# Preparing a stage's first weights, bias and input inside the stage before it, in tiles that stage has used up

## The chip, the cores and the metric

The kernel runs on one core of a Trainium2 chip. The metric is device time in microseconds (us) of one execution. The engines are TensorE (PE; its weight loads are PEld), VectorE (DVE), ScalarE (ACT), GpSimd (POOL) and SyncE (SP); SP issues nearly all transfers, in order. Each engine takes its instructions in one fixed order and waits on semaphores.

## The reference

Two transformer-like layers over one sequence of 4096 rows and 256 channels, in float32. What matters here is layer 0, and that layer 1 follows it.

```
x = L0_attn_x                                  # (1, 4096, 256)
sa, ca, ga, sb, cb, gb = modulation(L0_c)      # six rows of 256
h = layernorm(x) * (1 + ca) + sa
x = x + ga * attention(h)                      # 16 heads of 16, causal; ... @ Wo + bo
h = layernorm(x) * (1 + cb) + sb
shared = swiglu(h @ w_shared_in) @ w_shared_out
probs  = softmax(h @ w_gate + gate_bias)       # 8 experts, the top 2 kept as weights wd
hid    = swiglu(h @ w1_shared)
x = x + gb * (shared + sum_e wd[e] * (hid @ w2[e]))
... layer 1: a gated delta rule and a quantised matmul ...
```

The constants `ga` and `gb` are folded into weights by the kernel: `Wo` and `bo` are multiplied by `ga`, `w_shared_out` and `w2` by `gb`.

## The kernel before

**Stages.** Setup computes the modulation rows on PE and DVE (pool `modw`). The attention follows (`attention`, L249): `attn_inputs` goes through 8 blocks of 512 rows, normalises them, forms queries, keys and values, and writes queries and keys to DRAM in high and low parts; then `interleave` (L309) runs 32 steps, each one group g of 4 heads with one block T of 512 queries. After that the mixture (`mixture`, L672) and layer 1.

**Keys in the attention.** `kts[i][p]` (L255) are four tiles of 128x4096: group g's keys are in `kts[g % 2]`, p is the pair of heads. So `kts[0]` holds groups 0 and 2, `kts[1]` groups 1 and 3. The steps are laid out in the list at L276 to L280; the last six are (3,2), (3,3), (3,7), (3,6), (3,5), (3,4), all with group 3, and group 2's last step is (2,4) just ahead of them. All four tiles and the values `vall` are filled with a constant by POOL (L256 to L259), then the causal mask is brought by a transfer that POOL issues (L264) and copied twice by DVE (L268).

**A step.** PE forms logits for row maxima (tile `m`, two buffers), DVE reduces them (`mx`, L526, one 128x1024 tile at a time), the maxima go back as query rows through SP (`q<-mrow`), and PE forms the logits again (`e`), ACT takes the exponential (L640), PE multiplies with the values (`o`). Maxima run ahead of the steps that need them; the query loads (`q<-qd`) run four steps ahead. At a step's end `ot` is copied by ACT, transposed, and divided by DVE (`rec`, `o`, L659 and L660).

**The mixture.** `mixture_weights` (L704) loads all weights and the input into new tiles and prepares them. Weights that must be exact are split in two halves by `halves` (L692): DVE cuts the low bits away (`cut`, L696), ACT copies the high part, POOL subtracts to get the low part (L700). That is done for `w_shared_in` and `w1_shared` (tile `win`) and for 8 pieces of `w2` (tile `w2f`, two buffers), each piece multiplied by `gb` first (L745). POOL also adds the bias to every block of x (`biased`, L772). `before_experts(b)` (L751) makes for one block of 512 rows: the heads' transposes, the projection with `Wo` and its sum into x (L789), statistics with a root on POOL (L798), normalisation on ACT (L804), transposes, gate and the choice of two experts (`chosen`), and 8 products for the two hidden layers. `experts(b)` does the shared product and 4 pairs of experts for each of 4 tiles of 128 rows, on PE, and DVE adds them into x (L911, L927). Block b + 1's pieces are mixed into block b's experts by a list of slots.

**What sets the order.** Python order is program order. A scheduler places instructions on each engine by a simulated clock and by program order as priority; what goes through `mm`, `tp`, `mma` (PE) and `dv` (mostly DVE) keeps its program order among itself, the rest may be moved ahead as far as its inputs and buffers allow. A pool opened after another is closed may take the same bytes, and then the first use waits for the last use of what lay there. The wait is by pool: in the program before, the pool `attn` lies at bytes 56352 to 162592 of each partition and `modw` at 23584 to 56480; `kt00` itself lies at 93088.

**Layer 1** begins with some 20 loads on SP (from `Wq`), 24 DVE operations that make `conv` matrices, a quantised weight turned by PE (L1086), and the first block's normalisation, whose transposes (L1143) follow on PE.

Of the kernel before, what the change touches and what calls it, by code (L numbers as in the profile page):

```python
# [7 lines left out]
F32 = mybir.dt.float32  # L8
# [9 lines left out]
P = 128  # L18
# [81 lines left out]
class _Net:  # L100
# [150 lines left out]
    def attention(self):  # L251
# [3 lines left out]
        self.kts = [[self.t(ap_, [P, S], f"kt{i}{p}", F32R) for p in range(2)] for i in range(2)]  # L255
# [26 lines left out]
        with ExitStack() as c:  # L282
# [7 lines left out]
            self.small = e(tc.tile_pool(name="asmall", bufs=2))  # L290
            self.ps_e = e(tc.tile_pool(name="ps_e", bufs=3, space=PSUM))
# [24 lines left out]
    def interleave(self):  # L316
# [16 lines left out]
        values, tail = None, None  # L333
        for i, (g, T) in enumerate(steps):
# [5 lines left out]
            ahead(need[i])  # L340
            for n, (logits, made) in enumerate(self.weighted(g, T)):
# [8 lines left out]
                values = made  # L350
        values(0)
# [321 lines left out]
    def mixture(self):  # L673
        nc, tc = self.nc, self.tc
        with ExitStack() as c:
# [5 lines left out]
            self.mixture_weights()  # L681
            for f in self.before_experts(0):
                f()
            for b in range(NB):
# [7 lines left out]
    def halves(self, full, high, low, ordered=True):  # L692

        nc = self.nc
        cut = self.t(self.ms, [P, 512], "cut")
        ins = nc.vector.tensor_scalar(cut.bitcast(I32), full.bitcast(I32), HIGH, None, ALU.bitwise_and)  # L696
        if ordered:
            self.dv(ins)
        nc.scalar.copy(high, cut)
        nc.gpsimd.tensor_tensor(low, full, cut, ALU.subtract)  # L700

    def mixture_weights(self):
        nc, a, wp = self.nc, self.a, self.mw
        m = self.mods[0]  # L704
        w = self.w = {}
        xs = a["L0_attn_x"].rearrange("o (n p) c -> p (o n) c", p=P)

        def load(b):
            nc.sync.dma_start(out=self.x[:, 4 * b : 4 * b + 4, :], in_=xs[:, 4 * b : 4 * b + 4, :])

        w["o"] = self.weight(wp, a["L0_attn_Wo"], C, "wo")
        load(0)
        bo = self.rows(wp, a["L0_attn_bo"], C, "bo")

        nc.vector.tensor_tensor(
            w["o"], w["o"], m["ga"].unsqueeze(1).to_broadcast([P, 2, C]), ALU.mult
        )
        nc.vector.tensor_tensor(bo, bo, m["ga"], ALU.mult)
        w["bo"] = bo
        w["g"] = self.weight(wp, a["L0_ffn_w_gate"], 8, "wg")  # L720
        w["gbias"] = self.rows(wp, a["L0_ffn_gate_bias"], 8, "gbias")
        w["in"] = []
        for name, tag in (("L0_ffn_w_shared_in", "wsi"), ("L0_ffn_w1_shared", "w1s")):
            full = self.t(self.ms, [P, 2, 512], "win")
            nc.sync.dma_start(out=full, in_=a[name].rearrange("(k p) n -> p k n", p=P))
            t = self.t(wp, [P, 2, 2, 512], tag, F32R)
            for k in range(2):
                self.halves(full[:, k], t[:, 0, k], t[:, 1, k], ordered=False)
            w["in"].append(t)

        w["so"] = self.weight(wp, a["L0_ffn_w_shared_out"], C, "wso")
        nc.gpsimd.tensor_tensor(
            w["so"], w["so"], m["gb"].unsqueeze(1).to_broadcast([P, 2, C]), ALU.mult
        )
        gb2 = m["gb"].unsqueeze(1).to_broadcast([P, 2, C])
        w["2"] = self.t(wp, [P, 2, 2, 8, C], "w2", F32R)
        for k in range(2):
            for e in range(0, 8, 2):
                es = slice(e, e + 2)
                full = self.t(self.ms, [P, 2, C], "w2f")  # L740
# [7 lines left out]
        for b in range(1, NB):  # L748
            load(b)

    def before_experts(self, b):  # L751
# [22 lines left out]
        def attended(k):  # L774
# [4 lines left out]
            if k == 0 and b == 0:  # L779
                biased(0)  # L780
# [920 lines left out]
```

## Time and profile before

| | us |
|---|---|
| median of 3 runs (lowest, highest) | 3238.63 (3233.23, 3240.27) |
| the profiled execution | 3230.99 |
| its span | 3229.2 |
| busy: PE, DVE, ACT, POOL | 2924.4, 2239.3, 1786.7, 454.0 |
| granted TensorE clock, mean | 0.907 of full speed |
| last reduction step's `rec` of group 2 (step (2,4)) | at 1511.13 |
| attention's last `ot` copy | at 1834.64 |
| first expert pair of the mixture | 1907.63 to 1909.16 |
| last expert product of the mixture | to 2234.8 |

Busy times say which engine works most, not what holds the end. The chain of waits does that: followed back from the last instruction, it names at each time what the next piece of work waited for. The timeline shows each engine's instructions in order of time, with the idle time before them and what ended it. The table by windows shows the same stretch for all engines, with the clock granted to PE.

### The profile page before, as it was taken

The numbers are of one execution on the slowest core, as the hardware profiler recorded it, in microseconds if no ns is written. First come the engines' busy times: TensorE is split into PE (matmuls) and PEld (weight loads), VectorE is DVE, ScalarE is ACT, GpSimd is POOL, SyncE is SP. The second block draws the span as 40 slices with busy tenths as digits, with TensorE's granted clock in tenths as the row PEclk, the third lists the DMA queues.
The fourth block names the chain that finished last, engine by engine and source line by source line (L and its number), as shares of the span: only waits on it lengthen the run. The fifth ranks groups of instructions, "written<-read, shape, count | busy, mean of one in ns | idle before, by whom it ended". The sixth has DMA issues, their size and how long they took to land.

```text
span 3229.2 us, 61627 instructions
## 1 busy us (share of the span) xinstructions
PE 2924.4 (91%) x24988; PEld 1740.1 (54%) x24988; DVE 2239.3 (69%) x3923; ACT 1786.7 (55%) x3866; POOL 454.0 (14%) x698
## 2 busy tenths in 40 slices
PE   4877999999999999999999769997788998889877
PEld 3444444444444444444444358886667677667755
DVE  4565688888888888888887266666247557755665
ACT  0211577777877777777888622221555455545521
POOL 3222100000000000000000141111223223323312
PEclk8777799999999999999999979998889798989855
DMA  3433100003000020000000110001011011101000
GB/s 123 140 129 110 30 10 11 12 7 51 7 12 12 13 49 6 12 10 8 11 2 2 52 49 1 1 1 27 10 19 19 11 24 22 20 13 23 18 19 11
DMA packets 143084, 89.05 MB, mean 28 GB/s; under 512 B 102928, under 2 KB 120848, under 8 KB 142224
## 3 DMA queue, kind: packets, MB, share of 16 engines
q1 hardware_dynamic: 142656, 85.04, 10.3%
q8 instruction: 197, 3.23, 0.4%
q14 instruction: 87, 0.71, 0.1%
q0 software_dynamic: 144, 0.07, 0.0%
HBM read 51.05 MB, written 33.55 MB: 26 GB/s over the span
## 4 chain that ended last, share of the span: by engine, by line
PE 67%; DVE 19%; ACT 6%; issue 3%; POOL 3%; DMA 2%; SPq 1%; DVEq 0%; POOLq 0%; ACTq 0%
PE o L168 16%; PE e L168 13%; DVE mx L526 9%; PE m L168 9%; PE f L1152 9%; PE b L1152 6%; PE a L1152 4%; PE f L168 2%; PE w L168 2%; DVE step L1384 1%; ACT kk L1281 1%; PE ps L427 1%; DVE T L1391 1%; ACT e L640 1%; DVE by L1246 1%
## 5 line engine op out<-in xcount | busy, mean ns | idle before, releaser
L640 ACT ACTIVATE e<-e 128x512 f32<-128x512 f32 (+1 forms) x2176 | 1151.5, 583 | 319.6 <-PE e L168 285.7
L526 DVE TENSOR_REDUCE mx<-m 128x2 f32<-128x1024 f32 (+3 forms) x1088 | 1202.0, 1129 | 171.2 <-PE m L168 158.9
L168 PE MATMUL o<-e,vall 128*32 128x256 f32 (+2 forms) x9216 | 692.4, 375 | 5.4 <-ACT ot L617 5.4
L168 PE MATMUL e<-q,kt 50*128 50x512 f32 (+3 forms) x2688 | 571.3, 438 | 0.3 <-ACT e L640 0.3
L168 PE MATMUL m<-kt,q 48*128 48x512 f32 (+3 forms) x2688 | 481.1, 379 | 7.4 <-DVE mx L526 4.9
L168 PEld LDWEIGHTS e<-q,kt 50*128 50x128 f32 x2688 | 249.9, 185 | 431.8 <-issue 257.8
L168 PEld LDWEIGHTS o<-e,vall 128*32 128x32 f32 x9216 | 192.5, 108 | 323.8 <-issue 300.6
L168 PEld LDWEIGHTS m<-kt,q 48*128 48x128 f32 x2688 | 249.9, 192 | 85.4 <-issue 45.4
L772 POOL TENSOR_TENSOR x<-x,bo 128x1024 f32<-128x1024 f32 x8 | 19.9, 2505 | 1508.3 <-DMA x<-in_L_attn_x_dram 1508.3
L1152 PE MATMUL f<-conv,pT 128*128 128x128 f32 x1536 | 224.4, 297 | 0.0
L1152 PEld LDWEIGHTS f<-conv,pT 128*128 128x128 f32 x1536 | 200.8, 206 | 8.7 <-issue 1.4
L1152 PE MATMUL b<-w,hid 128*128 128x512 f32 x768 | 195.9, 399 | 0.0
L927 DVE SCALAR_TENSOR_TENSOR x<-b,wd,x 128x256 f32<-128x256 f32 x256 | 123.6, 483 | 66.5 <-PE b L1152 59.4
L1152 PEld LDWEIGHTS b<-w,hid 128*128 128x128 f32 x768 | 143.3, 188 | 29.9 <-POOL hid L700 0.3
L1475 ACT ACTIVATE gs<-S,gm 128x64 f32<-128x64 f32 x256 | 75.4, 340 | 117.6 <-DVE S L1503 117.3
L534 DVE TENSOR_REDUCE mx<-m 128x8 f32<-128x1024 f32 x64 | 78.4, 1225 | 71.0 <-PE m L168 70.6
L1503 DVE TENSOR_TENSOR S<-gs,w 128x128 f32<-128x128 f32 x128 | 36.5, 285 | 126.7 <-PE w L168 104.3
L168 PE MATMUL w<-S,uw 64*32 64x64 f32 x1024 | 62.8, 252 | 54.8 <-DVE S L1503 53.9
L1480 DVE TENSOR_TENSOR ut<-uw,w 32x256 f32<-32x256 f32 x128 | 53.3, 416 | 80.9 <-PE w L168 79.1
L1384 DVE TENSOR_TENSOR step<-T,Ls 128x126 f32<-128x126 f32 (+22 forms) x248 | 79.4, 320 | 27.1 <-DMA Ls<-dL 21.9
L1152 PE MATMUL f<-frac,hT 128*128 128x128 f32 x640 | 90.9, 295 | 0.0
L168 PEld LDWEIGHTS w<-S,uw 64*32 64x32 f32 x1024 | 38.6, 122 | 94.8 <-DVE S L1503 70.1
(286 smaller groups left out, 3636.3 us busy)
## 6 DMA issues: line engine op xcount, KB each, us to landing
q<-qd SPq DMA_DIRECT2D x128, 96.0 KB
kt<-kd SPq DMA_DIRECT2D x12, 768.0 KB
x<-in_L_attn_x_dram SPq DMA_DIRECT2D x16, 512.0 KB
kd<-high SPq DMA_DIRECT2D x32, 256.0 KB
qd<-high SPq DMA_DIRECT2D x32, 256.0 KB
kd<-full SPq DMA_DIRECT2D x16, 256.0 KB
qd<-full SPq DMA_DIRECT2D x16, 256.0 KB
Ls<-dL SPq DMA_DIRECT2D x64, 64.0 KB
```

Source lines behind the costliest of these rows:

```text
L168: self.nc.tensor.matmul(out, lhsT, rhs, start=start, stop=True, skip_group_check=skip)
L427: nc.tensor.matmul(ps, w[:, k, ch * P : (ch + 1) * P], hT[:, k, :], start=(k == 0), stop=(k == 1))
L526: nc.vector.tensor_reduce(mx[:, 2 * pair : 2 * pair + 2, s, col], ps[:, :, at : at + w], AX.X, ALU.max)
L534: nc.vector.tensor_reduce(mx[:, 2 * pair : 2 * pair + 2, :, 0], ps.rearrange("p h (s k) -> p h s k", k=P), AX.X, ALU.max,)
L640: nc.scalar.activation(e[:, 0:at], ps[:, 0:at], AF.Exp)
L927: nc.vector.scalar_tensor_tensor(x, ps[:, e, :], wd[:, s, n : n + 1], x, ALU.mult, ALU.add)
L1152: self.nc.tensor.matmul(out, lhsT, rhs, start=(k == 0), stop=(k == n - 1))
L1246: nc.vector.tensor_tensor(by[z].rearrange("p (i h) f two -> p i (h f) two", i=2), qk.rearrange("p i h (f two) -> p i (h f) two", two=2), c ...
L1384: nc.vector.tensor_tensor(step[:, 0:m, 0:n], T[:, 0:m, j].unsqueeze(2).to_broadcast([P, m, n]), Ls[:, j + 1 : 32, j].unsqueeze(1).to_broad ...
L1475: nc.scalar.activation(gs[:, pair, :], state[:, pair, :], AF.Identity, scale=gm[:, pair, c : c + 1])
L1480: nc.vector.tensor_tensor(ut[rows].rearrange("p (a b) d -> p a b d", b=2), u[rows].rearrange("p (a b) d -> p a b d", b=2), pw[rows, :, 0:1 ...
L1503: nc.vector.tensor_tensor(self.state, gs, pw[:, 0, 128:256].rearrange("p (a d) -> p a d", d=64), ALU.add)
```

## The change

Keys tiles `kts[0]` move from the attention's pool to the pool `heads`, which stays open through the mixture. When group 2 is finished, these tiles take the mixture's first data:

- `mixture_vectors` loads the gate's weights and bias into the constants' pool, and puts `Wo`, `w_shared_out`, `bo` (each multiplied on POOL) and the first block of x with `bo` added into `kts[0][1]`. Each goes through a tile `full` of a new pool `early` (two buffers): load, POOL operation, transfer into place.
- `mixture_early` returns four pieces that split `w_shared_in` and `w1_shared` into `kts[0][0]`: load, DVE cut, ACT copy, POOL subtraction.
- In the mixture, blocks 1 to 7 of x are loaded first, and the eight splits of `w2` (`split_expert`) are written out between the pieces of the first `before_experts`, after `chosen`. `w2` has two tiles, one per k.
- The bias of block b + 1 is added after `chosen(b)`, in program order; the first block's sum reads x and bias from `kts[0][1]`.

```diff
-        self.kts = [[self.t(ap_, [P, S], f"kt{i}{p}", F32R) for p in range(2)] for i in range(2)]
+        self.kts = [[self.t((self.hp, ap_)[i], [P, S], f"kt{i}{p}", F32R) for p in range(2)] for i in range(2)]
...
+            self.early = e(tc.tile_pool(name="early", bufs=2))
...
+        later, count = [], 0
...
             ahead(need[i])
+            if i == len(steps) - 4:
+                self.mixture_vectors()
+            if i == len(steps) - 2:
+                later = self.mixture_early()
...
+                count += 1
+                if later and count % 3 == 0:
+                    later.pop(0)()
+        for f in later:
+            f()
...
-            self.mixture_weights()
-            for f in self.before_experts(0):
+            xs = self.a["L0_attn_x"].rearrange("o (n p) c -> p (o n) c", p=P)
+            for b in range(1, NB):
+                nc.sync.dma_start(out=self.x[:, 4 * b : 4 * b + 4, :], in_=xs[:, 4 * b : 4 * b + 4, :])
+            self.w["2"] = [self.t(self.mw, [P, 2, 8, C], f"w2{k}", F32R) for k in range(2)]
+            for n, f in enumerate(self.before_experts(0)):
                 f()
+                if 9 <= n < 13:
+                    for k in range(2):
+                        self.split_expert(self.ms, k, 2 * (n - 9))
...
+    def mixture_vectors(self):
+        nc, a, cp = self.nc, self.a, self.const
+        m = self.mods[0]
+        room = self.kts[0][1].bitcast(F32)
+        wo, wso = (room[:, 512 * n : 512 * n + 512].rearrange("p (k n) -> p k n", k=2) for n in range(2))
+        self.x0 = x0 = room[:, 1024:2048].rearrange("p (s n) -> p s n", s=4)
+        bo = room[:, 2048:2304]
+        self.w = {"o": wo, "so": wso, "bo": bo}
+        self.w["g"] = self.weight(cp, a["L0_ffn_w_gate"], 8, "wg")
+        self.w["gbias"] = self.rows(cp, a["L0_ffn_gate_bias"], 8, "gbias")
+
+        def kept(to, src, shape, op, by):
+            t = self.t(self.early, [P, 512], "full")
+            flat = t[:, 0 : shape[0] * shape[1]]
+            wide = flat.rearrange("p (k n) -> p k n", k=shape[0])
+            nc.sync.dma_start(out=wide, in_=src)
+            nc.gpsimd.tensor_tensor(wide, wide, by.unsqueeze(1).to_broadcast([P, *shape]), op)
+            nc.sync.dma_start(out=to, in_=wide)
+
+        kept(wo, a["L0_attn_Wo"].rearrange("(k p) n -> p k n", p=P), (2, C), ALU.mult, m["ga"])
...
+        for n in (0, 2):
+            kept(x0[:, n : n + 2, :], xs[:, n : n + 2, :], (2, C), ALU.add, bo)
+
+    def mixture_early(self):
...
+                pieces.append(lambda i=i, k=k, src=src: self.split(src, w["in"][i][:, 0, k], w["in"][i][:, 1, k]))
+        return pieces
+
+    def split(self, src, high, low):
+        nc = self.nc
+        full = self.t(self.early, [P, 512], "full")
+        nc.sync.dma_start(out=full, in_=src)
+        cut = self.t(self.early, [P, 512], "cut")
+        nc.vector.tensor_scalar(cut.bitcast(I32), full.bitcast(I32), HIGH, None, ALU.bitwise_and)
         nc.scalar.copy(high, cut)
         nc.gpsimd.tensor_tensor(low, full, cut, ALU.subtract)
...
+    def split_expert(self, pool, k, e):
+        nc, w = self.nc, self.w
+        src = self.a["L0_ffn_w2"][e : e + 2, k * P : (k + 1) * P, :].rearrange("e p c -> p e c")
+        full = self.t(pool, [P, 512], "full")
+        nc.sync.dma_start(out=full.rearrange("p (e c) -> p e c", e=2), in_=src)
...
+        nc.vector.tensor_tensor(wide, wide, gb2, ALU.mult)
+        cut = self.t(pool, [P, 512], "cut")
+        nc.vector.tensor_scalar(cut.bitcast(I32), full.bitcast(I32), HIGH, None, ALU.bitwise_and)
+        high, low = (w["2"][k][:, h, e : e + 2].rearrange("p e c -> p (e c)") for h in range(2))
+        nc.scalar.copy(high, cut)
+        self.dv(nc.gpsimd.tensor_tensor(low, full, cut, ALU.subtract))
...
-            self.dv(nc.vector.tensor_tensor(xh, ps, xh, ALU.add))
+            two = slice(2 * half, 2 * half + 2)
+            old = x4 if b else self.x0
+            self.dv(nc.vector.tensor_tensor(x4[:, two, :], ps, old[:, two, :], ALU.add))
...
-            nc.gpsimd.tensor_tensor(rs, ve, self.mhalf[:, 0:4], ALU.pow)
-            biased(b + 1)
+            self.dv(nc.gpsimd.tensor_tensor(rs, ve, self.mhalf[:, 0:4], ALU.pow))
...
             self.dv(nc.vector.tensor_tensor(wd, pr, picked, ALU.mult))
+            biased(b + 1)
...
     with tc.tile_pool(name="heads", bufs=1) as hp:
+        net.hp = hp
```

## The prediction

> **What bounds the kernel now.** I read the page's overview first: PE is busy for 2924 us of a 3229.2 us span, so I looked for the places where it is not. The chain of waits and the timeline, read around the lines of the diff, show two holes, one at the start and one between attention and mixture.
>
> The chain of waits, start of the span (start, us, what). From 34.4 to 59.3 us the chain is POOL filling tiles, a small transfer and two DVE copies; PE waits.
>
> ```profile
> 34.41 13.94 POOL kt L258 x4
> 48.34 7.64 POOL vall L259
> 55.99 2.40 DMA causal<-in_const_causal_dram
> 58.41 0.49 DVE mask L268 x2
> 58.91 0.33 DVE x L148
> 59.29 2.20 PE ps L158 x8
> ```
>
> The same view from the attention's end (1834.6) to the experts. PE's first projection ends at 1842.13, and nothing of PE's is on the chain until 1886.6: the holder is the weights' splitting, three near-equal rounds of load, multiply, cut and subtract, 8.67 us apart (1854.60, 1863.27, 1871.94).
>
> ```profile
> 1838.31 7.17 DMA wso<-_L_ffn_w_shared_out_dram
> ...
> 1854.60 2.72 DMA w2f<-in_L_ffn_w_dram
> ...
> 1857.41 1.64 DVE w2f L745
> ...
> 1859.14 2.39 DVE cut L696
> ...
> 1861.60 1.65 POOL w L700
> 1863.27 2.51 DMA w2f<-in_L_ffn_w_dram
> ...
> 1882.25 0.60 DVE x L789
> ...
> 1890.26 15.63 PE a L1152 x62
> ...
> 1907.63 1.53 PE b L1152 x6
> ```
>
> The table by windows gives the granted clock (after POOL's busy time, ahead of the DMA share): half speed after the hole, full speed again only from about 1896.
>
> ```profile
> 1842.00:1844.00 2.00, 0.13 (x1) 0.00 (x0) 0.00 (x0) 0.00 (x0) 1.22 (x1) 1.00 1.05 398
> 1846.00:1848.00 2.00, 0.00 (x0) 0.00 (x0) 1.10 (x1) 0.57 (x2) 2.00 (x2) 0.50 1.09 346
> 1894.00:1896.00 2.00, 2.00 (x7) 1.52 (x6) 1.46 (x9) 1.51 (x2) 0.00 (x0) 0.50 0.00 0
> 1896.00:1900.00 4.00, 4.00 (x18) 3.29 (x17) 2.26 (x10) 1.20 (x2) 0.00 (x0) 0.95 0.00 0
> ```
>
> The DVE timeline late in the attention, where the new splits land: ten reductions back to back, 1.24 us each, no gap.
>
> ```profile
> 1512.03 12.39 DVE L526 TENSOR_REDUCE mx<-m 128x2 f32<-128x1024 f32 x10 [0.19 <-PE m L168]
> ```
>
> The timeline of PE at layer 1's start: its first matmul there, after 16.45 us of waiting.
>
> ```profile
> 2251.22 0.59 PE L1086 MATMUL f<-identb,wqb 128*128 128x128 bf16 x4 [16.45 <-issue]
> ```
>
> **Part 1, the start.** Moving kt00 and kt01 out of the attention's pool changes more than it says. In the memory map of the program before, that pool begins at byte 56352 and shares 128 bytes with the modulation's pool, which ends at 56480, so its first fill waits for the modulation (34.4). After, the pool begins at 89216 and shares none. POOL's order in the built kernel is now kt10, kt11, vall, the causal load and both mx without that wait, and only then kt00 and kt01 with it. From about 0.4 us: two fills at 3.49 (13.94 / 4) and vall at 7.64 end near 15; the masks' transfer (2.40) ends near 18. What stays behind 34.41 is two fills, 6.98, to 41.4.
> On DVE, beside a fill, a TENSOR_SCALAR of 128x2 at 34.38 lasted 3.56 us, to that fill's end, and one of 128x4 at 39.33 lasted 2.09, to 41.42, while bn_stats ran through. In the new order the two mask copies stand ahead of that first TENSOR_SCALAR. If neither is held, POOL's root starts at 41.5 and the normalised x at 42.6 instead of 58.82: 16.2 us. If the second copy (due at 34.45, just after the fill begins) is held to 37.9, the TENSOR_SCALAR is held to 41.4, the block's statistics (four times 0.39 and 0.15, then 0.16: 2.3) end at 43.7, the root (1.02) at 44.8: 14.0 us. No row has a copy beside a fill; the nearest row, that TENSOR_SCALAR, was held, so I take 14.0.
> The Trainium skill (SBUF — State Buffer, SBUF: two separate sides) says that DVE and GpSimd share one port pair, held for a whole instruction, and that a copy in a two-port mode is among those that wait. By that rule too the gain is 14.0 and the sum below 38.0; without it 16.2 and 40.2.
> The early fills also stand beside DVE's copy of scb (9.67): held to 15.1 it is still ahead of its reader on PE (16.68): 0. Everything up to the keys' loads follows the first block, with no clock of its own: the gain stays.
>
> **Part 2, preparation inside the attention.** POOL gets five multiplications or additions and four subtractions (1.26 to 1.44 each), in a stretch where it has nothing: 0. The SP queue gets nine loads and five stores. Two loads stand behind the first keys' loads, ahead of query loads that wait for later logits; two stores and two loads stand between 1490 and 1503, where SP has nothing else (issues at 1487.55 and 1503.47): 0. The rest stand behind the four query loads that end at 1505.7 and ahead of those at 1533.93. The store of bo, the second x load, two x stores and the piece loads form a series: taking 2.5 us each (the w2f rows) and 1.3 to 1.5 for each POOL step between, the first two pieces land near 1515.9 and 1517.9, and the last near 1523.4, before 1533.93: no query load is late, 0.
> DVE reaches its first cut after two reductions, at 1514.5: a wait of 1.4. Then four cuts of 0.43 (1904.07 has one alone): 3.1 in all, in the stretch without gaps. An m tile is written again 2.48 after its last writing began and is free after 0.45 + 1.23: 0.8 of slack. So 2.3, and 0.2 for semaphores: **2.5 lost**. ACT's four copies (0.57 to 0.62, 2.4) fall in the same 10 us, where ACT has 1.8 us idle (8.19 busy of 10) plus PE's delay: covered. Bounds: 0 if the transfers are quicker and PE's lead larger, 6 if the wait is 4 or cuts are held by POOL (2.39 was seen).
>
> **Part 3, the hole.** Removed from ahead of the first block: four cuts of win, eight multiplications and cuts of w2, and POOL's eight subtractions with its biases. The first x sum's second half had its input at 1842.13 and began at 1882.25. After, DVE has two gb multiplications in front (loads issued at 1834.7 and 1835.2, landed by 1837.8, 0.68 each), done by 1839.3; so it starts at 1842.2, and all to the hidden matmuls moves 40.1 us forward: 1893.27 becomes 1853.2. That is the upper bound.
> But the experts' eight splits now stand behind, in DVE's queue between the hidden blocks' products, and their loads pass through two buffers. Step by step: the first cut (after lg, 1853.4) shares its time with POOL's bias of block 1 (2.34) and ends at 1855.0; POOL's two subtractions (1.3 each) end at 1856.6 and 1858.3; the selection's 16 small DVE operations (0.225 from start to start) end at 1860.2. Then three rounds, each load 2.7, multiply 0.68, cut 0.43, subtract 1.3, semaphores 0.2, thus 5.3: with the first delayed by the selection, subtractions 3, 5, 7 end at 1863.0, 1868.4, 1873.7, and DVE's eighth cut at 1874.9. Behind it wait hid0's second product (0.69), both sl products (0.69) with their cuts (0.43): 2.9 to 1877.9, since the last PSUM tiles were filled by 1867.5. POOL's two subtractions end at 1879.6, and the first expert pair ends near 1880.6 instead of 1909.16: 28.5.
> PE stands still from 1867.5 to 1875.7. Row: 2 to 4 us after 1842.13 the clock was 0.50, and it took unbroken work from 1890.26 to about 1896.2 to be full again. The same at half speed costs 2.9. The Trainium skill (TensorE: Matmul & The Clock Gate, Part 1: The HAM clock gate) gives one activity window of about 3.4 us; by it the loss is an estimated 1.7 (half of it) and the sum below would be 39.2. I take the row: 28.5 - 2.9 = **25.6 gained**. Bounds: with the old rounds of 8.67 each, 3 x 3.4 = 10.1 less, 15.5; without the clock's loss, 28.5.
> The biases of blocks 1 to 7 (2.34 each) were done in the hole; now one per block runs on POOL. Cover: POOL's 2.6 to 3.6 busy of 20 us in steady state; the cuts they may hold feed hid tiles used a block later: 0. If that cover failed, at most 7 x 2.34 = 16.
>
> **Part 4, layer 1.** Its weight tiles now lie where kt0 and o lay, and the first load waits for the last shared product (2228.26 to 2229.28) and not for the last expert pair (2234.8): 5.6 earlier. DVE's conv stretch (from 2241.98, waiting for taps) then starts when x and three tiles' statistics are done, 2237.5: 4.5 earlier, ending at 2247.7. But the fourth tile's statistics, the root and the first nxn now stand behind it: 0.36 + 0.30 + 0.17 + 1.01 + 0.16 + 0.52 and gaps, 2.9, to 2250.6; the transposes began at 2251.6. **0.9 gained**, bounds -2 and 4.5.
>
> **Sum.** 14.0 + 25.6 + 0.9 - 2.5 = 38.0. The profiled execution took 3230.99 (span 3229.2), so 3193.0. It is 7.6 below the median of the runs, 3238.63; for the median I say 3238.6 - 38.0 = **3200.6**.
>
> **Rivals.**
> A, the splits keep their old rounds (8.67): DVE's multiplications took 1.64 and cuts 2.39 beside POOL. Against: that was beside POOL's x biases (5.08 for two), mostly gone. 10.1 less: 3210.7.
> B, the start gives nothing, another wait taking the fill's place (the weights' loads, or kt00's fill before the first key load). Against: all those loads are issued by 18.2. 38.0 - 14.0 = 24.0: 3214.6.
> C, the attention's DVE waits a whole transfer (2.5) at each of four cuts: 10 more lost, 3210.6. The built order puts one or two reductions (1.24) between cuts, which speaks for half of that at most.
> D, slower: the clock. After the shorter pause PE's full clock could be throttled through the mixture, which is PE alone for 327 us (1907.6 to 2234.8). It decides from 38 us of loss, a clock of 327 / (327 + 38) = 0.90; at 0.85 it costs 57.7: 3258. Against: the page's granted clock is 9 tenths or more in every slice from 404 to 1857, without a pause.
>
> **How the numbers follow.** Forecast 0.62, A 0.18, B 0.08, C 0.08, D 0.03, a remainder within 0.2% 0.01. The likeliest case alone spans 3194 (16.2, 28.5, 4.5 at the start, hole and layer 1, less 5) to 3208. The range reaches A, C and part of B: 3190 to 3215. Within 0.2% (6.5 us, near what runs from 3233.23 to 3240.27 can tell) is 0.01, slower 0.03, faster 0.96.
>
> **What would show it.** Right: POOL's vall fill near 7 us and the first PE transposes at 43 to 45; ten reductions near 1500 stretched by 3 with four cuts among them; x's first sum right after its projection; three rounds of about 5.3 in the splits, PE idle for about 8 us before the experts at half clock; layer 1's first load ahead of the last pairs. Wrong: rounds over 7, a gap on PE in the attention over 6, blocks of the mixture longer than 40.9 us ((2234.8 - 1907.6) / 8), or a clock below 1.00 there.

## The result and the profile after

The changed kernel took 3188.43 us (median of 4 runs, 3182.70 to 3194.45), the kernel before 3236.78 beside it (4 runs): a ratio of 0.9851, 95% interval 0.9829 to 0.9873, so 48.4 us less. The prediction was 3200.6 with a range from 3190.0 to 3215.0; the time lies 1.6 us below the range, in the case that was forecast. The profiled execution took 3182.70 (span 3180.9) against 3230.99 (span 3229.2): 48.3 less.

The table sets both profiles side by side; the times are starts of the first or last instruction of a tile. "Again" columns are further profiles of the same two kernels, taken in the experiments.

| us from the span's start, or length of a stage | before | again | after | again | third |
|---|---|---|---|---|---|
| modulation's last row (`gb`, L242) starts | 33.80 | 30.89 | 29.95 | 29.97 | 30.17 |
| first transposes of the attention | 59.3 | 56.6 | 39.3 | 39.4 | 39.6 |
| from there to the attention's first division | 293.6 | 294.6 | 293.6 | 293.6 | 293.4 |
| first to last division of the attention | 1483.0 | 1483.0 | 1486.2 | 1485.9 | 1507.7 |
| last division to first hidden product | 57.3 | 57.3 | 16.9 | 16.9 | 16.9 |
| first hidden to first expert product | 14.1 | 14.2 | 26.1 | 26.1 | 26.1 |
| first to last expert product | 327.0 | 327.0 | 327.5 | 327.5 | 328.4 |
| last expert product to layer 1's first Wq product | 23.0 | 23.1 | 22.7 | 22.3 | 22.3 |
| from there to the end | 971.8 | 970.9 | 968.4 | 967.1 | 971.5 |

The chain of waits of the changed kernel, start of the span. The fills of 34.41 to 55.99 are gone from it; what is left of them are two DVE operations that last 3.23 and 2.00 us beside the two late fills.

```profile
19.64 3.53 PE pc L206 x32
...
29.95 0.41 DVE gb L242
30.36 0.40 DVE mask L269 x2
...
31.00 3.23 DVE bq L421
...
35.71 2.00 DVE ave L145
37.80 1.05 POOL ars L133
38.87 0.42 DVE x L148
39.34 2.20 PE ps L158 x8
```

POOL's timeline shows where those fills went: three start at once, two after the modulation.

```profile
0.73 6.96 POOL L259 MEMSET kt<- 128x4096 f32 x2 [0.29 <-POOLq L1719]
7.62 7.84 POOL L260 MEMSET vall<- 128x9184 f32 x1
...
30.55 7.13 POOL L259 MEMSET kt<- 128x4096 f32 x2 [13.92 <-issue]
```

The chain between attention and experts. The first sum into x has its second half at 1825.31, where PE's projection of 1821.49 (3.79 long) ends. What holds the experts is two rounds of load, multiply, cut and subtract that begin at 1848.88 and 1855.05, on to DVE's last cut and the hidden product behind it.

```profile
1825.31 0.70 DVE x L823
...
1848.88 2.59 DMA full<-in_L_ffn_w_dram
...
1855.05 2.62 DMA full<-in_L_ffn_w_dram
...
1858.60 0.43 DVE cut L780
1859.03 0.61 DVE hid L911
1859.68 1.22 PE b L1186 x2
```

PE's timeline there, and the table by windows (the granted clock stands after POOL's busy time): PE pauses for 6.50 us, and the clock is 0.50 until about 1862.9.

```profile
1859.68 1.22 PE L1186 MATMUL b<-kt,hid 128*128 128x256 f32 x2 [6.50 <-DVE hid L911]
```

```profile
1854.00:1856.00 2.00, 0.00 (x0) 0.00 (x0) 0.65 (x1) 0.32 (x1) 1.03 (x1) 1.00 0.37 118
1856.00:1858.00 2.00, 0.00 (x0) 0.00 (x0) 0.70 (x3) 0.62 (x1) 1.29 (x1) 0.50 0.49 131
...
1860.00:1862.00 2.00, 2.00 (x9) 1.71 (x9) 1.76 (x4) 0.96 (x2) 1.53 (x2) 0.50 0.00 0
...
1864.00:1866.00 2.00, 2.00 (x10) 1.75 (x11) 0.97 (x2) 0.07 (x1) 0.00 (x0) 1.00 0.03 8
```

In the attention, DVE's first early cut waits 1.77 us for its piece (DVE's timeline), and PE then waits 1.19 (PE's timeline).

```profile
1496.62 0.43 DVE L766 TENSOR_SCALAR cut<-full 128x512 int32<-128x512 int32 x1 [1.77 <-DMA full<-n_L_ffn_w_shared_in_dram]
```

```profile
1498.24 0.50 PE L168 MATMUL e<-q,kt 50*128 50x512 f32 x1 [1.19 <-ACT e L652]
```

Layer 1's first load is issued at 2184.74, ahead of the last expert products (2189.8), and the first Wq product follows the last expert product by 22.7 instead of 23.0.

So the first profiled pair adds up as: start 20.0, attention -3.2, hole 27.8 (40.4 less before the hidden products, 12.0 and 0.5 given back behind them), layer 1's start 0.3, layer 1's body 3.4. The sum of the prediction had 14.0, -2.5, 25.6, 0.9 and nothing for layer 1's body.

### The profile page after: what moved, and what is told of

Read it like the earlier page. It is cut to its first block, busy times and chain, and to the rows that moved or that the text cites. A ratio compares the mean times of both kernels' runs of the same rounds, so it can differ in the third digit from the quotient of the medians.

```text
span 3180.9 us, 61656 instructions
## 1 busy us (share of the span) xinstructions
PE 2918.7 (92%) x24988; PEld 1732.8 (54%) x24988; DVE 2239.9 (70%) x3921; ACT 1786.7 (56%) x3866; POOL 452.4 (14%) x701
## 3 DMA queue, kind: packets, MB, share of 16 engines
q8 instruction: 197, 3.23, 0.4%
## 4 chain that ended last, share of the span: by engine, by line
PE 66%; DVE 19%; ACT 6%; issue 3%; POOL 2%; DMA 2%; SPq 1%; DVEq 0%; POOLq 0%; ACTq 0%
PE o L168 16%; PE e L168 13%; PE m L168 9%; DVE mx L538 9%; PE f L1186 9%; PE b L1186 6%; PE a L1186 4%; PE f L168 2%; PE w L168 2%; DVE step L1418 2%; ACT kk L1315 1%; DVE T L1425 1%; PE ps L439 1%; ACT e L652 1%; DVE by L1280 1%
## 5 line engine op out<-in xcount | busy, mean ns | idle before, releaser
L961 DVE SCALAR_TENSOR_TENSOR x<-b,wd,x 128x256 f32<-128x256 f32 x256 | 123.5, 482 | 61.8 <-PE b L1186 55.3
L1186 PE MATMUL a<-hs,kt 128*128 128x512 f32 x384 | 102.7, 406 | 2.2 <-DVE hid L911 2.2
```

The lines of the kernel that those rows point to most:

```text
L961: nc.vector.scalar_tensor_tensor(x, ps[:, e, :], wd[:, s, n : n + 1], x, ALU.mult, ALU.add)
L1186: self.nc.tensor.matmul(out, lhsT, rhs, start=(k == 0), stop=(k == n - 1))
```

## The experiments

Theory: the gain comes from the three places named, and what exceeds the sum is partly chance of those executions. Rivals: each of the surplus terms belongs to the change; or a place gives nothing and another gives more.

**The same two kernels again.** No edit.

> The kernel before, unchanged, profiled again. Two terms of the sum stay open: PE's second pass of column products in the modulation (32 products) took 6.62 us before and 3.53 after, and layer 1 from its first Wq product to the end took 971.8 us before (3229.2 - 2257.40) and 968.4 after (3180.9 - 2212.49). Theory 1, both vary from one execution to the next whatever the kernel: here the pass takes anything from 3.5 to 7.0, and layer 1 anything from 967 to 973. Theory 2, both belong to the program: the pass takes 6.6 again, and layer 1 971.8 within 0.5.

> The changed kernel, unchanged, profiled again. Theory 1 (the pass's speed and layer 1's 3.4 us vary from one execution to the next): the pass takes anything from 3.5 to 7.0, the first transposes start between 39 and 43, layer 1 takes 967 to 973. Theory 2 (they belong to the program): 3.53, 39.3 and 968.4 within 0.5. By both, PE's pause ahead of the experts is 6.5 again within 0.5.

The kernel before took 3228.41, and its second column pass 3.69 instead of 6.62; its layer 1 took 970.9. The chain of waits of this second profile:

```profile
20.51 3.69 PE pc L206 x32
...
30.89 0.43 DVE gb L242
...
31.50 13.94 POOL kt L258 x4
```

The changed kernel took 3188.11 (4 runs, ratio 0.9866, 0.9837 to 0.9896), with a pass of 3.51 and a layer 1 of 967.1. Theory 1 holds for the pass: one and the same kernel before has 6.62 and 3.69, and two profiles of another unchanged kernel below have 6.62 and 3.54. Over all 15 profiles of the study it is 6.6 to 7.0 in eight and 3.5 to 3.8 in seven. The modulation's end, 3.85 us earlier in the first pair, is therefore no gain of the change (3.09 of it is this pass; 0.66 is the first pass's start, 9.69 against 9.03, which lies anywhere from 8.98 to 9.96 in the 15 profiles). For layer 1 the third profile decides: 971.5 in a changed kernel, as before, and the kernel before with a pad, below, has 968.4. Its 3.4 us are chance too.

**The start alone.** 128 bytes in the kernel before, so that the pools no longer touch.

```diff
         net.o = net.t(hp, [P, NT, C], "o")
+        net.t(hp, [P, 32], "pad")
```

> The kernel before with one tile of 128 bytes behind the heads, so that the attention's tiles share no byte with the modulation's; nothing else. My theory (the shared 128 bytes alone held the fills): all four key fills and vall run from 0.7 to about 22.5, the first transposes start at 35 to 39 instead of 59.29 (fills free from the start: 33.8 for the end of the modulation at full speed or 4 later, 2.3 of statistics, 1.05 for the root, 0.5), and 20 to 24 us are gained, unless DVE's copy of scb is held by the fills to 15 or 22 and PE's row products with it (then 6 less). Rival, another wait takes the fills' place: transposes after 50, gain under 10.

3209.77 us (ratio 0.9926, 0.9902 to 0.9950): about 24 us of 3233. The chain of waits:

```profile
20.11 6.62 PE pc L206 x32
...
33.61 0.42 DVE gb L242
...
38.25 0.38 DVE x L148
38.67 1.56 PE ps L158 x5
```

With the slow pass, the transposes still start at 38.67 instead of 59.29, 20.6 earlier. So the 128 bytes held all fills (the addresses of the memory map stand in no profile; that a pad of 128 bytes is enough is what this run shows), and an edit of one line, which leaves every tile in its pool, gains more at the start than the change does: here no fill stands beside the statistics.

**The start undone.** The changed kernel with its fills, mask load and `mx` behind the modulation's last row.

```diff
+        late = self.mods[1]["gb"][:, 0:1]
+        nc.gpsimd.tensor_copy(self.vall[:, 0, 0:1], late)
+        for kt in self.kts[1]:
+            nc.gpsimd.tensor_copy(kt[:, 0:1], late)
...
+        nc.gpsimd.tensor_copy(causal[:, 0:1], late)
...
+            nc.gpsimd.tensor_copy(m[:, 0, 0, 0:1], late)
```

> The changed kernel with all fills, the mask's load and mx made to wait again for the modulation's last row (tiny POOL copies of it into each tile first), the rest as changed. My theory, the start's gain adds to the rest: the first transposes start at 53 to 59.3 (POOL fills 21.6 us from 30.4 or 34.2 on), so 14 to 20 us of the 48 are lost and the kernel takes 3202 to 3209. Rival, the later parts hide the start (something late in the kernel ends by its own clock): less than 5 lost, 3188 to 3193.

3204.28 us (7 runs; ratio 0.9916, 0.9891 to 0.9941): 16.2 above the changed kernel of the same call, inside the 14 to 20. The first transposes start at 58.11. The start's gain adds to the rest.

Its profiled run took 3227.36, and the surplus lies in the attention's last step. The table by windows:

```profile
1788.00:1792.00 4.00, 4.00 (x40) 1.82 (x34) 0.00 (x0) 3.19 (x9) 0.00 (x0) 1.00 0.00 1
1792.00:1796.00 4.00, 3.52 (x23) 1.40 (x22) 0.45 (x2) 2.65 (x6) 0.00 (x0) 0.56 0.01 4
```

From 1796 PE is busy almost without a break and works at half clock to the attention's end near 1860. That was in no theory; more of it below.

**Four load buffers in the hole.**

```diff
-        full = self.t(pool, [P, 512], "full")
+        full = self.t(pool, [P, 512], "full", bufs=4)
```

> The changed kernel with four buffers for the loads of w2's splits instead of two. In the changed kernel two runs took 26.2 and 26.0 us from the first hidden product to the first expert product, 6.5 of them PE's pause. My theory, each round of 5.3 is a round trip through the two load buffers (load 2.6, multiply, cut, subtract, next load): with four, the fifth to eighth load start two subtractions earlier, DVE's eighth cut comes at about 1849 instead of 1858.6, the pause goes and the stretch takes 19 to 21: 5.5 to 7 us gained, about 3182. Rival, DVE and POOL themselves set the rounds (multiply 0.68, cut 0.43, subtraction 1.3, each holding the other): 24 to 26, under 2 gained.

The first hidden to the first expert product took 20.0 us instead of 26.1: 6.1 gained, as my theory had it, against under 2 by the rival. The eighth cut came 16.3 us after the first hidden product instead of 22.5 (the theory had 12.9), and instead of one pause of 6.50 PE has short ones (PE's timeline):

```profile
1858.21 3.02 PE L1186 MATMUL a<-hs,kt 128*128 128x512 f32 x12 [1.11 <-DVE hid L911]
...
1866.03 0.70 PE L1186 MATMUL b<-kt,hid 128*128 128x256 f32 x2 [1.71 <-DVE hid L911]
```

The time, 3185.57 (0.9872, 0.9834 to 0.9911; runs from 3178.54 to 3206.86), is too scattered to show the 6 us. The profiled run's attention took 1493.7 instead of 1486, although nothing was changed there. Its windows show why: behind the first division the clock was still at 0.50 for 25.2 us, to 363.3, with PE busy in all of that time; in the changed kernel it was so for 7.5, to 340.5.

**The w2 splits ahead of the first block.**

```diff
-            for n, f in enumerate(self.before_experts(0)):
-                f()
-                if 9 <= n < 13:
-                    for k in range(2):
-                        self.split_expert(self.ms, k, 2 * (n - 9))
+            for e in range(0, 8, 2):
+                for k in range(2):
+                    self.split_expert(self.ms, k, e)
+            for f in self.before_experts(0):
+                f()
```

> The changed kernel with the eight splits of w2 put back ahead of the first block's pieces; weights, bias and first x stay prepared early. From the attention's last division to the first expert product it took 71.4 us before and 43.1 after. My theory, both parts count, and the splits ahead delay the first sum into x by about 16 us while they take PE's later pause away: 33 to the first hidden product and 14.5 from there, 47.5 in all, 4 to 5 us slower than the changed kernel. Rival 1, the splits' place is the whole gain of the hole: 71 again, 28 slower. Rival 2, their place does not matter since they must be made anyway: 43 within 1.

41.3 us to the first hidden product and 14.0 from there: 55.3, 12.3 worse than the changed kernel; the time was 3206.55 (5 runs; 0.9929, 0.9905 to 0.9953). Both rivals fall. My estimate of 47.5 was 7.8 too low, and the chain of waits shows what most of that is:

```profile
1841.61 7.87 DMA full<-in_L_ffn_w_dram
...
1854.17 2.59 DMA full<-in_L_ffn_w_dram
```

The third and fourth pieces were queued behind the seven blocks of x, and took 7.87 instead of 2.6, which is 5.3. Of the 28 us that the hole lost, some 12 hang on the splits' place; the other 16 are left for weights, bias and x being ready, by subtraction, since no run changed these alone.

**The early cuts late.** `cut` in `split` kept in program order, so that it stands in the last two steps.

```diff
-        nc.vector.tensor_scalar(cut.bitcast(I32), full.bitcast(I32), HIGH, None, ALU.bitwise_and)
+        self.dv(nc.vector.tensor_scalar(cut.bitcast(I32), full.bitcast(I32), HIGH, None, ALU.bitwise_and))
```

> The changed kernel with the four early cuts of DVE kept in program order, which puts them between the reductions of the attention's last two steps instead of around 1500. From the first to the last division of the attention it took 1483.1 and 1483.0 before, 1486.2 and 1485.9 after. My theory, the 3 us are DVE's cuts and waits among reductions that PE waits for: 1483 within 0.7 if the last steps' reductions run ahead of their use by more than the cuts, about 3185.5. Rival, the cost comes from the stage's transfers and POOL work: 1486 within 0.5.

The attention's stage took 1483.9, 2.2 less than with the early cuts and 0.9 above the kernel before, a little outside the 0.7. The transfers and POOL's work stayed, so DVE's cuts and the wait in front of them are most of the loss (the second profile of this kernel, below, has 1483.3). Time 3185.56 (0.9884, 0.9832 to 0.9936), with one run of four at 3213.95.

**The fills free of both.** Group 0's key tiles in a pool of their own behind a pad, filled by ACT.

```diff
+        net.t(hp, [P, 32], "pad")
+        net.hp = kp = keep.enter_context(tc.tile_pool(name="keys0", bufs=1))
...
+        for kt in self.kts[0]:
+            flat = kt[:, :]
+            some = self.mods[0]["sa"][:, 0:1].to_broadcast([P, S])
+            nc.scalar.activation(flat, some, AF.Identity, bias=1.0, scale=0.0)
+        for kt in self.kts[1]:
+            nc.gpsimd.memset(kt.bitcast(F32), 1.0)
```

> The changed kernel with group 0's key tiles in a pool of their own that shares no byte with the modulation, and filled by ACT instead of POOL, so that no fill stands beside DVE's first statistics. In the changed kernel the first transposes start 8.98 us after the modulation's last row (30.36 to 39.34), 5.3 of it DVE operations held to a fill's end (3.23 and 2.00). My theory: 4 to 5 us instead of 8.98, the transposes at 34.5 to 35.5 if the modulation ends near 30.4 (38 to 39 if near 34), 4 to 5 gained, about 3184. Rival, another wait takes the place (ACT's fills late for the first keys, or the statistics behind the mask): 8 to 9 again.

From the modulation's last row to the first transposes: 34.25 to 38.64, 4.4 us instead of 9.0. The held operations take 0.08 now (chain of waits):

```profile
34.89 0.08 DVE bq L424
...
36.94 0.08 DVE ave L145
...
38.17 0.42 DVE x L148
```

So 4.6 us of the start are left in the changed kernel by the two late fills. The time, 3193.40 (0.9895, 0.9870 to 0.9921), does not show it; one run was at 3209. In the profile the attention took 1488.6 instead of 1486, with 15.1 us at half clock in it instead of 7.5.

**PE made busy ahead of the modulation.**

```diff
+            zero = self.t(wp, [P, P], "zero")
+            nc.vector.memset(zero, 0.0)
+            warm = self.t(pp, [P, P], "warm")
+            for _ in range(18):
+                nc.tensor.matmul(warm, zero, zero, start=True, stop=True)
```

> The changed kernel with 18 products of a zero tile put on PE ahead of the modulation, in the first 9 us in which PE waits for its first input; their result is used by nothing. So far the modulation's first pass of 32 column products took 6.98 or 6.99 in every profile, the second 3.51 to 3.69 in some and 6.62 in others, of the kernel before and the changed one alike. My theory, the pass is at half clock until PE has worked for a while: after 7 us of other work the first pass takes about 3.5, and the second 3.5 too; the modulation's last row comes about 3.5 earlier than in the two profiles of the changed kernel, at 27, unless vall's fill, which holds DVE's copy of scb to 15.6, keeps PE's row products there (16 as before, then nothing is gained, but the second pass is 3.5). Rival, the passes' times belong to the products themselves or to their weights' arrival: 7 and 3.5 to 6.6 again.

The first pass took 4.57 instead of 6.98, the second 3.71 (PE's timeline):

```profile
1.08 6.46 PE L191 MATMUL warm<-zero 128*128 128x128 f32 x36 [1.08 <-DVE zero L188]
9.82 4.57 PE L211 MATMUL pc<-sc,wm 128*128 128x1 f32 x32 [2.28 <-ACT sc L201]
...
19.23 3.71 PE L211 MATMUL pc<-sc,wm 128*128 128x1 f32 x32
```

The passes' time follows PE's work before them, not the arrival of their weights; the windows have the clock at 0.50 from 12.5 to 19.4, from the middle of the first on, and without that it would have taken an estimated 3.6 (2.7 at full speed and half of the other 1.9). The row products were still held to 15.6 with `scb` by vall's fill, as expected, and the modulation's last row came only 1.5 earlier, at 28.41. Even that was lost again: the first transposes started at 40.65 instead of 39.34, 11.8 after the last row's end and not 9.0. POOL's and DVE's timelines show the reason. The fill began 0.06 ahead of the two mask copies, and both copies, 0.28 each in the changed kernel, lasted 3.6 each, to the end of a fill.

```profile
29.02 7.11 POOL L264 MEMSET kt<- 128x4096 f32 x2 [12.38 <-PE pr L230]
29.08 7.20 DVE L274 COPY mask<-causal 128x512 bf16<-128x512 bf16 x2
```

The time was worse, 3199.89 (0.9910, 0.9882 to 0.9939), and the profile says why, elsewhere: DVE's first early cut waited 3.01 for its piece, PE then 2.43, and the clock fell to 0.50 from 1504 to 1572. The attention's stage took 1514.5. DVE's timeline, PE's and the windows:

```profile
1500.57 0.43 DVE L771 TENSOR_SCALAR cut<-full 128x512 int32<-128x512 int32 x1 [3.01 <-DMA full<-n_L_ffn_w_shared_in_dram]
```

```profile
1502.20 0.50 PE L168 MATMUL e<-q,kt 50*128 50x512 f32 x1 [2.43 <-ACT e L657]
```

```profile
1500.00:1504.00 4.00, 1.80 (x15) 0.75 (x15) 3.43 (x5) 2.95 (x6) 1.53 (x2) 1.00 0.38 91
1504.00:1508.00 4.00, 4.00 (x26) 1.40 (x24) 3.42 (x4) 2.84 (x6) 2.29 (x2) 0.51 0.39 111
...
1568.00:1572.00 4.00, 4.00 (x28) 1.40 (x24) 2.13 (x3) 2.00 (x4) 0.00 (x0) 0.50 0.02 4
1572.00:1576.00 4.00, 4.00 (x44) 1.37 (x36) 3.54 (x4) 2.87 (x7) 0.00 (x0) 0.95 0.00 0
```

The other profiles with early cuts show how the fall goes with the pause. Behind PE's pause of 0.68 (start undone), 1.19 and 1.18 (the changed kernel twice) and 1.29 (four buffers) the clock stayed at 1.00; behind 1.27 (splits ahead) it was 0.50 for 31 us (the next expectation has 36, which is too much), behind 1.29 (free fills) for 3.

**A pause on purpose.** The late cuts, and two DVE operations without use among the reductions of steps (3,2) and (3,3).

```diff
+            if i == len(steps) - 6:
+                idle = self.t(self.early, [P, 2560], "idle", bufs=1)
+                self.dv(nc.vector.memset(idle, 0.0))
+            if i == len(steps) - 5:
+                self.dv(nc.vector.tensor_tensor(idle, idle, idle, ALU.mult))
```

> The kernel with the early cuts in program order (so without the wait of DVE for the first piece among the reductions), and in its place one DVE operation without use: a 128x2560 filling among the reductions of step (3,2) and a 128x2560 multiplication among those of step (3,3), 3.4 us by the multiplications of 128x512 (0.68 each). In seven profiles DVE's wait for the first early piece left PE idle for 0.68 to 1.29 us, in one for 2.43; in three of these eight the granted clock fell to 0.50 right behind the pause, for about 3, 36 and 68 us, which cost up to 28 us. My theory, PE's pause is what brings the clock down: a pause of over 2 us on PE at the multiplication, clock 0.50 right behind it, the attention's stage (first to last division) at 1490 to 1515 instead of 1484, and a median 5 to 25 above the 3185.6 of the kernel without these operations. Rival, the falls come by chance wherever PE works: clock 1.00 behind the pause, 1484 plus the pause itself, 1485 to 1488.

> The early cuts in program order, as before, unchanged: four runs gave 3181.4, 3183.1, 3188.0 and 3214.0. My theory: median 2.5 to 6 us under that of the changed kernel run beside it (the pause's 2.6, and the falls of the clock behind it that some runs of the changed kernel have), and the profile shows the clock at 1.00 from 1400 to the attention's end. Rival, falls of the clock come as often without the pause: median the same as the changed kernel's within 2, and at least two of six runs over 3190.

> The changed kernel, unchanged. Theory: PE idle for about 1.2 us at the first early cut again; a median of 3185 to 3190 and a span from lowest to highest of 10 us or more, since some runs have the clock fall behind that pause; if the profile has it, the attention's stage takes over 1486. Rival: a spread of under 6 us, so that the earlier spread had another cause.

The two operations took 2.19 and 2.81 us, PE paused for 2.26 and 2.15, and with both the clock fell: at 1496.5, still in the pause, for 7 us the first time, at 1534.1 for 55 the second. PE's timeline with both pauses, and the windows around the second:

```profile
1497.55 0.80 PE L168 MATMUL m<-kt,q 48*128 48x512 f32 x2 [2.26 <-DVE mx L544]
...
1532.27 0.50 PE L168 MATMUL m<-kt,q 48*128 48x512 f32 x2 [2.15 <-DVE mx L544]
```

```profile
1530.00:1532.00 2.00, 0.12 (x2) 0.00 (x0) 2.00 (x2) 1.53 (x4) 0.00 (x0) 1.00 0.01 4
...
1534.00:1536.00 2.00, 1.48 (x10) 0.92 (x12) 1.89 (x4) 0.96 (x2) 0.00 (x0) 0.53 0.00 0
...
1588.00:1590.00 2.00, 2.00 (x20) 1.17 (x17) 0.00 (x0) 1.13 (x4) 0.00 (x0) 0.82 0.04 8
```

The attention's stage took 1515.8 (0.8 over the expected span), and the median was 3206.22 (4 runs, 3199.80 to 3216.88) against 3182.89 for the same kernel without the two operations (5 runs, 3181.75 to 3187.73) and 3190.81 for the changed kernel (6 runs, 3182.92 to 3208.29): 5.0 us of DVE work cost 23. My theory holds in that a pause of over 2 us brought the clock down three times of three. The late cuts came out 7.9 under the changed kernel, more than the 2.5 to 6 expected, with no run of five above 3188, and the profile shows the clock at 1.00 from 1400 to the attention's end, as expected. The changed kernel has a spread of 25, as its expectation had it (10 or more), and a median 0.8 above the 3185 to 3190.

But the rival is not gone. The third profile of the changed kernel, of one of its two longest runs (3207.76), had a pause of only 0.44 at the cuts, where 1.2 was expected, and no fall there; its clock fell at 1774, behind a wait of 0.47 for `ot` that every kernel has, and its stage took 1507.7. The same happened in the profile of the start undone, two of 15 profiles in all, and the late cuts' run at 3213.95 has no profile. So falls come by chance as well, rarely; a pause of PE of over 2 us makes them likely. For pauses of 1.2 the counts, two of five, are too small to say.

**Three mends together.** Four load buffers, late cuts, free fills, as in the diffs above.

> The changed kernel with four buffers for w2's loads, the early cuts kept in program order, and group 0's key tiles in a pool of their own filled by ACT. If the three gains seen one by one add (6.0 from the first hidden to the first expert product, 2.2 to 3 in the attention, 4.6 from the modulation's last row to the first transposes): 12.5 to 13.5 us in these stages, a median near 3175, so 0.4% under the changed kernel. If one takes the other's place (the cuts late in the attention delay the first hidden products, or the fills): the stage from the last division to the first expert product takes over 39 instead of 37, and under 9 us in all.

3176.96 us (5 runs, 3174.44 to 3179.15; ratio 0.9832, 0.9818 to 0.9847), 13.3 below the median of all 14 runs of the changed kernel, 3190.3. The stages: 4.4 us from the modulation's last row to the transposes, 1485.4 in the attention (the late cuts alone had 1483.3 and 1483.9), 16.9 and 20.1 behind it. The gains of start and hole add. The attention's is there too, under the clock. The windows of this run and of the late cuts' second profile, 6 to 11 us behind the first division in each:

```profile
340.00:344.00 4.00, 4.00 (x22) 1.85 (x22) 1.23 (x1) 1.66 (x3) 0.00 (x0) 0.50 0.02 5
```

```profile
340.00:344.00 4.00, 3.84 (x37) 1.65 (x35) 2.45 (x2) 1.67 (x4) 0.00 (x0) 0.92 0.03 7
```

From the first division on, the clock is at 0.50 for 11.6 us in this profile, and for 7.5 or 7.6 in both profiles of the kernel before, in all three of the changed one and in both of the late cuts. The 4.1 more cost an estimated 2.0, half of them, which leaves 1483.3. The kernel before with the pad has 11.7 there and a stage of 1484.6: 1482.5 by the same estimate, against 1483.0.

## Why the prediction was right and where it was wrong

**What holds over many runs.** All runs of the kernel before in the study, 42 in five comparisons, have a median of 3231.3 (3224.4 to 3242.5); 14 of the changed kernel have 3190.3 (3180.5 to 3208.3): 41.0 less. The stages that repeat from profile to profile give nearly the same: 16.1 at the start, -3.1, 27.8 and 0.6, together 41.4. So the sum of 38.0 was some 3 short, and the three places and their signs were as told. The step that failed by most is the last one, "for the median I say 3238.6 - 38.0": the median of three runs was taken for the base, and 42 runs put it at 3231.3, 7.3 lower. Why the first runs lay high is not known. The forecast of 3200.6 is therefore 10.3 above the 3190.3 of all runs, 7.3 by the base and 3.0 by the sum; the first comparison's four runs lay another 1.9 lower, which is chance. The profiled execution, 3230.99, was the better base: the 3193.0 that the sum gave from it is 2.7 above the 3190.3. The range had no term for any of this: it was built from unknown costs of the edits alone, and the profile of one execution could not show what varies. In the second and third comparison the saving was 45.3 and 40.6, against 48.4 in the first; in the first profiled pair the modulation's end (3.85) and layer 1's body (3.4) had come out in favour of the change by chance.

**Part 1, the start: right mechanism, one step mis-sized.** The pool's 128 bytes, the new order of the fills and vall at 7.62 are as told; the pad alone and the start undone show that they are the whole gain. The step that failed is "if the second copy is held": I took 14.0 because an operation of another shape had been held. The mask copies ran from 30.28 to 30.76 and the fill began at 30.55, so the second copy had started 0.07 ahead of the fill and ran through beside it; nothing was held ahead of `bq`, and the end was the other one given, 16.2 (measured: 34.22 to 59.29 and 30.36 to 39.34, thus 25.1 less 9.0, 16.1). By the Trainium skill (SBUF — State Buffer, SBUF: two separate sides), of a GpSimd operation and a DVE operation in a two-port mode, whichever starts first has the shared ports for the whole instruction; the trace agrees, since the copies started 0.27 and 0.07 us before the fill and ran unhindered (this fill took 3.66, the next 3.53), while `bq` (0.15 alone) lasted 3.30 to the fill's end. The rule was right; the race's outcome was guessed. The run with PE made busy shows the other outcome: there the fill was 0.06 ahead, both copies were held, and the transposes came 11.8 after the last row, a gain of 13.3 instead of 16.1. So the 14.0 was a real branch of this race and not an impossible one; the eight other profiles with the change's fills went the way of the 16.1. `scb` was held to 15.6 (15.1 told), ahead of PE's product, which is on the chain from 16.01.

**Part 2, the attention: right.** 3.1 lost for 2.5. The first cut waited 1.77 (predicted 1.4), the cuts stand among ten reductions, no query load was late. Its upper bound of 6 is wrong: in the run where that wait was 3.01, the stage took 31 us more than in the kernel before, through the clock, which the text weighed for the mixture (rival D) and not here.

**Part 3, the hole: right but for the clock.** All to the hidden products moved 40.4 (40.1); the rounds took 5.39 and 5.36 (5.3), by the ends of subtractions 3, 5 and 7, though 6.2 and 5.4 by those of 4, 6 and 8, which the chain follows; PE paused for 6.5 (8.2). Net 27.8 against 25.6. The step that failed is the clock's loss of 2.9, taken from the row after the long pause of the kernel before (5.9 us at half speed). After the shorter pause PE worked at half clock for 3.2 us, from 1859.7 to 1862.9, so 1.6 lost; the other 0.9 is the rest of the step-by-step working, its pause of 8.2 above all. The Trainium skill (TensorE: Matmul & The Clock Gate, Part 1: The HAM clock gate) gives a window of about 3.4 that runs freely, so that the point of change varies; the trace agrees here, and the estimate of 1.7 worked out from it was nearer than my row. The biases cost next to nothing: 327.5 for the experts against 327.0 (the third profile's 328.4 begins with 3 us at half clock).

**Part 4, layer 1's start: right in kind.** 0.3 and 0.9 in two pairs of profiles (0.9); no run tested it alone.

**The rivals.** A fell (rounds of 5.4 to 6.2, not 8.67), B fell (both experiments on the start), C fell as a wait at each cut: only the first waited a transfer. D did not come: the mixture has full clock. Its mechanism exists, in the attention.

## What to carry to other kernels

Two pools that share 128 bytes made every first use in one wait for the last use in the other: look at the memory map before the order of the work. Before work is put into a stage that keeps PE full, ask how long PE would stand still if its input were late, not how long the added work takes. And before a sum is set against one profile or three runs, more runs and a second profile of the same kernel show how far the base moves, which stages repeat to 0.2 us and which wander by 3. Where a stage differs for no reason, compare its time at half clock first.

## What was not expected of the hardware

- A short pause can bring PE's clock to half for much longer than the pause: 2.26, 2.15 and 2.43 us of standing still in the attention's steps brought 7, 55 and 68 us at 0.50, although PE worked almost without a break; behind 1.18 to 1.29 us a fall came in two of five profiles, and at one wait of 0.47 in two of 15, where it is not shown that the wait is the cause. The Trainium skill (TensorE: Matmul & The Clock Gate, HAM oscillation — how this bites in real kernels) has the rule that no gap over about 3.4 us may arise; here smaller gaps were enough, and the measurement decides. In windows of 0.1 us the stretches at 0.50 that begin in the attention's steps and end there are 3.41, 6.83, 30.72, 54.61, 64.85 and 68.27 us long: 1, 2, 9, 16, 19 and 20 times 3.41. What sets the number stays open.
- The modulation's second pass of 32 column products took 3.5 to 3.8 or 6.6 to 7.0 in executions of one program, so 3 to 3.5 us of a run are drawn by lot in the first 25 us.
